# Two graph layers on one core: the first pair of tiles in one written order on four engines, with block-wise products and part of the weight sums on GpSimd

## The chip, the cores and the metric

The kernel runs on one core of a Trainium2 chip. The metric is the time of one execution on the device in microseconds (us), the median of several runs; lower is better. The engines are TensorE (PE), VectorE (DVE), ScalarE (ACT), GpSimd (POOL) and SyncE (SP, which here only issues DMAs). Each engine works through its own list of instructions in order and waits on semaphores for the others.

## The reference

x is 128 graphs of 64 rows with 768 columns, adj is 128 matrices of 64 x 64 zeros and ones. Two layers follow each other; the change touches only the first.

```
h = relu(layernorm(x))
# layer 0, with rels = heads = adj
ctx  = (adj @ (h @ Wadj.T + badj)) / deg + (adj.T @ (h @ Wrev.T + brev)) / rdeg
ctx += h @ Wself.T + bself
agg  = einsum('bij,bijr->bir', adj, E[rels])          # a gather from a table of 80 rows
rel  = agg @ Wr.T + br * deg + (the same with adj.T, E[rr], Wrr, brr)
x = x + ctx + rel
# layer 1
h = relu(layernorm(x))
x = x + gated graph attention of h (six heads of 128) under adj
```

Everything is float32. The gather is computed as a matrix of counts (how often each relation occurs in a row) times a table that already holds E times Wr and Wrr and the bias rows.

## The kernel before

The rows lie in 64 tiles of 128 rows (two graphs each), and two tiles are a pair. Layer 0 runs pair by pair. For each tile the normalised h is multiplied on PE by r, which holds the two scaled adjacencies and an identity: that gives the operands (`operands`, matmuls of line 566, copied out of PSUM by ACT, line 574), 3 blocks of 256 columns for each of the two tiles: a00, a01, a02, a10, a11, a12. They are multiplied by the weights B, a grid of 3 x 3 blocks b00 to b22, each holding its part of Wadj, Wrev and Wself. The result C has 2 x 3 blocks (tile, columns) and is added onto x by DVE (`add`, line 605).

Pair 0 computes C plainly, with 18 products (`PLAIN`); every later pair uses 15 products (`PRODUCTS`) of sums of the operands (f1 to f11, `form`, on DVE) and sums of the blocks of B (g1 to g14, u, v, w, `sum_of_weights`). The sums of B are formed once, while pair 0 runs: 13 operations over 128 x 1536 elements, all on DVE. Some are written over a block of B, and so have to wait until pair 0 is through with it. A product is six matmuls of 128 x 256 (line 613). Four PSUM banks, pwa to pwd, take the products; a bank is free again when DVE has added it onto x.

Around the products there is, for each pair: casting the adjacency (`prep`), degrees through a matmul (`degrees`, line 508) and their reciprocals (`over_degrees`, line 515, line 517 writes r), layer norm (`deviation`: statistics on DVE, the power -1/2 on POOL, line 282; `scaled_mean`, line 286, writes rn; `relu`, line 466, on ACT), the masks for counting (`prep_c`), the counts (`count`, two products over 128 x 1664 and a reduction, `digits`), three copies of them by POOL (line 545), their transposes on PE (`count_t`, line 553, copied out by ACT, line 555), and their product with the table (`counts`, line 597). `build_table` makes the table: `es` is the scaled E, six matmuls (lines 446 and 448) with wrt and the bias rows `bia` and `eb`, a copy by ACT (line 452), a split into three bfloat16 parts on DVE (lines 455 and 457), which DMAs lay into `tab`.

`merged(main, side)` interleaves a pair's list of matmul steps with side work at given step numbers. In layer 0 this gives priorities only: a scheduler in the compiler then orders each engine's instructions, except in a block `tc.manual_schedule(engines=...)`, where the named engines keep the written order. Before the change that holds for DVE alone, in a short stretch at the beginning (the casts and the norms of pair 0). Layer 1 is in a written order for PE, DVE, ACT and POOL (`ORDER`, `END`).

SP issues all loads. Its DMAs and those of ACT's queue share eight semaphores (lanes) in turn, and a DMA is issued only when the previous one of its lane has landed. Before the change the order on SP is: adjacency and x of pair 0, the blocks b00, b10, b20, b01, adjacency and x of pair 1, then b11, b21, b02, b12, b22, then wrt (2 x 384 KB), then the two small rows of `eb`.

Of the kernel before, what the change touches and what calls it, by code (L numbers as in the profile page):

```python
# [71 lines left out]

PLAIN = tuple((f"a{k}{j}", f"b{j}{q}", "abcdab"[2 * q + k], j == 0, f"{k}{q}" if j == 2 else None,
               "+", False) for q in range(3) for j in range(3) for k in range(2))

# [57 lines left out]
def kernel(  # L133
# [85 lines left out]
    def row(v, parts):  # L219

        n = 1
        for s in v.shape:
            n *= s
        return bass.AP(tensor=v.tensor, offset=v.offset, ap=[[0, parts], [1, n]])
# [12 lines left out]


    ident = const.tile([P, P], F32, name="ident")
    make_identity(nc, ident)  # L240
# [61 lines left out]

    def signed(to, s0, x, s1, y):

        if s0 == "-":
            return nc.vector.scalar_tensor_tensor(to, x, -1.0, y, op0=OP.mult,
                                                  op1=OP.add if s1 == "+" else OP.subtract)
        return (nc.vector.tensor_add if s1 == "+" else nc.vector.tensor_sub)(to, x, y)  # L308

# [8 lines left out]

    def sum_of_weights(places, n):
        s0, x, s1, y, at = B_SUMS[n]  # L320
        if at:
            places[n] = places[at]
        return signed(places[n], s0, places[x], s1, places[y])

# [30 lines left out]
    with ExitStack() as px:  # L355
# [5 lines left out]
        X, AI = {}, {}  # L361

        def load(p):
            if p >= NP:
                return
            AI[p] = work.tile([P, 2, 2, N], I32, name="ai")
            for d, src in ((0, adj), (1, adj_t)):
                nc.sync.dma_start(
                    AI[p][:, :, d, :],
                    src[p * 2 * GT : (p + 1) * 2 * GT].rearrange("(t g) i j -> (g i) t j", g=GT))  # L370
            for t in (2 * p, 2 * p + 1):
                X[t] = keep.tile([P, D], F32, name="x", bufs=6)
                nc.sync.dma_start(X[t], xf[t * P : (t + 1) * P, :])

        wrt = [keep.tile([P, D], F32, name="wrt", tag="x", bufs=6) for i in range(2)]
        load(0)
        et = wa.tile([P, NREL], F32, name="et")
        nc.scalar.dma_start(et, e_t)

        bia = keep.tile([5, D], F32, name="bia", tag="hf", bufs=2)  # L380
        for i, v in enumerate((br, brr, badj, brev, bself)):
            nc.scalar.dma_start(bia[i : i + 1, :], row(v, 1))


# [6 lines left out]

        for n in ("b00", "b10", "b20", "b01"):
            load_block(n)
        load(1)
        for n in ("b11", "b21", "b02", "b12", "b22"):
            load_block(n)
        nc.sync.dma_start(wrt[0], wr_t)
        nc.sync.dma_start(wrt[1], wrr_t)
        identb = wa.tile([P, P], BF16, name="identb")
        nc.vector.tensor_copy(identb, ident)  # L400

        blkb = wa.tile([P, P], BF16, name="blkb")
        nc.vector.memset(blkb, 0.0)
        for g in range(GT):
            s = slice(g * N, (g + 1) * N)
            nc.vector.memset(blkb[s, s], 1.0)

        vals = wa.tile([P, NG, N], BF16, name="vals")
        nc.gpsimd.iota(vals, pattern=[[1, NG], [0, N]], base=1, channel_multiplier=0,
                       allow_small_or_imprecise_dtypes=True)  # L410
        rts = []
        for i in range(2):
            r = wa.tile([P, 2, 3, N], F32, name=f"r{i}")
            for k in range(2):
                nc.vector.tensor_copy(r[:, k, 2, :], idc)
            rts.append(r)


        tabs = [wa.tile([3 * (b - a), D], BF16, name=f"tab{a}") for a, b in PARTS]

        def build_table():
            ids = wa.tile([P, NV], F32, name="ids")
            nc.gpsimd.iota(ids, pattern=[[1, NV]], base=1, channel_multiplier=0,
                           allow_small_or_imprecise_dtypes=True)
            es = wa.tile([P, 2, NROW], F32, name="es")
            nc.gpsimd.memset(es, 0.0)
            for d in range(2):
                nc.vector.tensor_mul(es[:, d, d * NV : (d + 1) * NV],
                                     et[:, d * NB + 1 : (d + 1) * NB], ids)


            eb = wa.tile([5, NROW], F32, name="eb")
            nc.gpsimd.memset(eb, 0.0)
            nc.gpsimd.iota(eb[0:1, 0:NV], pattern=[[1, NV]], base=1, channel_multiplier=0,
                           allow_small_or_imprecise_dtypes=True)
            ebr = wa.tile([1, NROW], F32, name="ebr")
            nc.gpsimd.memset(ebr, 0.0)
            nc.gpsimd.iota(ebr[0:1, NV:NCNT], pattern=[[1, NV]], base=1, channel_multiplier=0,
                           allow_small_or_imprecise_dtypes=True)
            nc.sync.dma_start(eb[1:2, :], ebr)  # L440
            nc.sync.dma_start(eb[2:5, NCNT:NROW], ident[0:3, 0:3])
            pt = pss.tile([P, 2, 512], F32, name="pb")
            for hf in range(2):
                s = slice(hf * HALF, (hf + 1) * HALF)
                for d in range(2):
                    nc.tensor.matmul(pt[:NROW, hf, :HALF], es[:, d, :], wrt[d][:, s],
                                     start=(d == 0), stop=False)
                nc.tensor.matmul(pt[:NROW, hf, :HALF], eb, bia[:, s], start=False, stop=True)
            v = keep.tile([P, D], F32, name="tv", tag="hf", bufs=2)
            qs = work.tile([P, 2, D], BF16, name="tq", tag="eq", bufs=1)  # L450
            ql = keep.tile([P, D], BF16, name="tl", tag="hf", bufs=2)
            nc.scalar.copy(v[:NROW].rearrange("p (a b) -> p a b", a=2), pt[:NROW, :, :HALF])
            for i in range(3):
                q = qs[:, i] if i < 2 else ql
                nc.vector.tensor_copy(q[:NROW], v[:NROW])
                if i < 2:
                    nc.vector.tensor_sub(v[:NROW], v[:NROW], q[:NROW])
                for (a, b), tab in zip(PARTS, tabs):
                    nc.sync.dma_start(tab[i : 3 * (b - a) : 3, :], q[a:b, :])
# [58 lines left out]

        def count(p, k):

# [4 lines left out]
            if p < 2 and k == 0:  # L525
                tc.keep_in_program_order(ins)
            nc.vector.tensor_tensor(
                eq, eq, WO[p][:, k, :, None, :].to_broadcast([P, 2, NG, N]), op=OP.mult)
# [55 lines left out]
        def main(p):  # L584
# [43 lines left out]

            rest_of = ["12"] if p else ["12", "01", "11", "10", "00", "02"]
            for i, c in enumerate(rest_of):  # L630
# [56 lines left out]

        with tc.manual_schedule(engines={mybir.EngineType.DVE}):
            prep(0)
            to = [small.tile([P, 2], F32, name="rn") for k in range(2)]  # L690
            mv = [small.tile([P, 2], F32, name="mv") for k in range(2)]
            deviation(X[0], to[0], mv[0])
            rd = degrees(0)
            scaled_mean(to[0], mv[0])
            over_degrees(0, rd)
            deviation(X[1], to[1], mv[1])
            scaled_mean(to[1], mv[1])
        for k in range(2):
            relu(k, to[k])
        operands(0, 0, 0)  # L700
        operands(0, 1, 0)
        prep_c(0)
        late = ([(8 + 6 * i, lambda k=k, q=q: operands(0, k, q)) for i, (k, q) in enumerate(
                    ((0, 1), (1, 1), (0, 2), (1, 2)))]
                + [(20, build_table), (22, lambda: count(0, 0)),
                   (24, lambda: count(0, 1)), (26, lambda: digits(0)),
                   (60, lambda: count_t(0, 0)), (60, lambda: count_t(0, 1))]
                + [(i, lambda n=n: sum_of_weights(bw, n)) for i, n in (
                    (21, "g10"), (38, "u"), (45, "g12"), (50, "g6"), (54, "g14"), (60, "v"), (75, "w"),
                    (85, "g3"), (88, "g9"), (91, "g5"), (94, "g8"), (97, "g1"), (100, "g11"))])  # L710
        for p in range(NP):
            more = [(3, lambda: [f() for k in range(2) for f in finish(p - 1, k)])] if p else late
            if p == 1:
                more.append((10, row_constants))
            if p == NP - 1:
                more += fetch()
            merged(main(p), own(p) + side(p + 1) + more)


    with ExitStack() as px:  # L720
# [366 lines left out]
        def parsed(order):  # L1087
            return [(n, int(k or 0)) for n, _, k in (x.partition("/") for x in order)]

        px.enter_context(tc.manual_schedule(engines={  # L1090
            mybir.EngineType.PE, mybir.EngineType.DVE, mybir.EngineType.Activation,
            mybir.EngineType.Pool}))
        ends = [f for k in range(2) for f in finish(NP - 1, k)]
# [61 lines left out]
```

## Time and profile before

| | |
|---|---|
| median of 5 runs | 2505.07 us (2504.53 to 2505.43) |
| the profiled execution | 2505.43 us |
| its span, first to last instruction | 2503.7 us |
| PE busy | 2465.6 us (98%), 12108 matmul records |
| DVE busy | 1975.4 us (79%) |
| ACT busy | 1073.2 us (43%) |
| POOL busy | 438.2 us (18%) |
| mean granted clock of PE | 0.995 |

A float32 matmul instruction stands as two records. In a timeline row the first number is the start in us from the beginning of the span, the second what the row took, then engine, line, operation, tiles (out <- in), shapes and number of records; in square brackets how long the engine was idle before and what released it. Ends of matmuls are modelled, so starts are the safer numbers there. In rows of windows the columns are: the window, its length, busy time of the engine, its granted clock, the share of the DMA engines' time, GB/s.

### The profile page before, as it was taken

To read this page: it belongs to the slowest core of one execution; us is meant where nothing else is said; L and a number is where in the kernel's file an instruction comes from. 1 tells how busy PE (TensorE), PEld (TensorE's weight loads), DVE (VectorE), ACT (ScalarE), POOL (GpSimd) and SP (SyncE) were. 2 spreads that over 40 slices of the span, in tenths; PEclk is the share of its full clock that TensorE was granted. 3 is DMA by queue.
4 is the path that set the end of the run, shared out by engine and by line. 5 is a ranking of instruction groups with operands and counts; after the bars stand their busy time and mean duration, and the time that the engine had idled before them with its cause. 6 is when DMAs were issued, how large, how long until landed. Compare 5 with 4: busy or idle time off the path is not lost. (4 is left out here: it accounts for less than half of the span.)

```text
span 2503.7 us, 35437 instructions
## 1 busy us (share of the span) xinstructions
PE 2465.6 (98%) x12108; PEld 1731.4 (69%) x12108; DVE 1975.4 (79%) x4112; ACT 1073.2 (43%) x3588; POOL 438.2 (18%) x799
## 2 busy tenths in 40 slices
PE   7999999999999999999999999999999999999997
PEld 5888888888888888888888884444444444444445
DVE  8978677777777776776777655888888888888888
ACT  2222222222222212222222213777777777777777
POOL 0122121121121211211211201111111111111112
PEclk9999999999999999999999999999999999999998
DMA  5122121121121121221211243344444444444434
GB/s 180 55 72 87 53 91 68 53 106 53 53 106 53 67 92 53 88 71 53 103 56 51 102 133 124 96 108 109 113 106 106 108 104 104 108 112 104 104 88 97
DMA packets 116216, 224.58 MB, mean 90 GB/s; under 512 B 36555, under 2 KB 49982, under 8 KB 116035
## 3 DMA queue, kind: packets, MB, share of 16 engines
q1 hardware_dynamic: 106152, 197.48, 24.2%
q0 software_dynamic: 9728, 24.78, 6.2%
q8 instruction: 95, 1.56, 0.3%
q14 instruction: 87, 0.70, 0.1%
q10 hardware_dynamic: 154, 0.06, 0.0%
HBM read 96.07 MB, written 100.66 MB: 79 GB/s over the span
## 5 line engine op out<-in xcount | busy, mean ns | idle before, releaser
L613 PE MATMUL pwa<-weights,op 128*128 128x256 f32 x2304 | 541.7, 382 | 1.1 <-DVE x L605 1.1
L613 PEld LDWEIGHTS pwa<-weights,op 128*128 128x128 f32 x2304 | 423.2, 190 | 69.1 <-DVE x L605 9.0
L574 ACT COPY op<-pb 128x768 f32<-128x768 f32 x160 | 124.2, 797 | 752.7 <-PE pb L566 752.7
L613 PE MATMUL pwb<-weights,op 128*128 128x256 f32 x1536 | 369.5, 381 | 0.0
L308 DVE TENSOR_TENSOR op<-op 128x768 f32<-128x768 f32 x248 | 231.6, 954 | 154.4 <-ACT op L574 154.3
L613 PEld LDWEIGHTS pwb<-weights,op 128*128 128x128 f32 x1536 | 284.5, 190 | 45.6 <-issue 7.0
L806 PE MATMUL pma<-weights,op_f 128*128 128x512 f32 x620 | 308.6, 595 | 1.9 <-DVE weights L833 1.9
L858 ACT ACTIVATE pr<-pr 128x128 f32<-128x128 f32 x768 | 225.3, 296 | 25.3 <-DVE pr L848 25.2
L282 POOL TENSOR_TENSOR rn<-ve,mhalf 128x1 f32<-128x1 f32 x128 | 107.1, 837 | 489.6 <-DVE ve L281 489.6
L806 PE MATMUL pmb<-weights,op_f 128*128 128x512 f32 x372 | 191.7, 597 | 0.0
L806 PEld LDWEIGHTS pma<-weights,op_f 128*128 128x128 f32 x620 | 112.2, 191 | 114.7 <-issue 104.5
L613 PE MATMUL pwc<-weights,op 128*128 128x256 f32 x780 | 187.1, 383 | 0.0
L613 PE MATMUL pwd<-weights,op 128*128 128x256 f32 x768 | 178.4, 381 | 0.0
L566 PE MATMUL pb<-r,h 64*128 64x192 f32 x1536 | 155.4, 341 | 10.2 <-DVE r L517 6.9
L613 PEld LDWEIGHTS pwc<-weights,op 128*128 128x128 f32 x780 | 145.8, 190 | 25.2 <-issue 6.7
L545 POOL COPY c<-cnt 128x243 bf16<-128x243 bf16 x64 | 44.9, 730 | 663.2 <-PE pb L553 598.7
L613 PEld LDWEIGHTS pwd<-weights,op 128*128 128x128 f32 x768 | 146.3, 191 | 20.3 <-issue 0.7
L566 PEld LDWEIGHTS pb<-r,h 64*128 64x128 f32 x1536 | 125.2, 189 | 46.4 <-issue 41.9
L276 DVE BATCH_NORM_STATS2 st<-x 128x6 f32<-128x384 f32 x256 | 134.7, 548 | 28.3 <-DMA x<-in_x_dram 27.1
L643 ACT ACTIVATE hf<-x,rn 128x768 f32<-128x768 f32 x64 | 65.8, 1027 | 192.7 <-issue 128.3
L858 ACT ACTIVATION_READ_ACCUMULATOR pr<-pr 128x1 f32 x768 | 144.2, 188 | 0.0
L645 POOL TENSOR_TENSOR x<-x,hf 128x768 f32<-128x768 f32 x64 | 115.9, 1811 | 92.7 <-ACT hf L643 92.6
(207 smaller groups left out, 4284.5 us busy)
## 6 DMA issues: line engine op xcount, KB each, us to landing
x<-in_x_dram SPq DMA_DIRECT2D x64, 384.0 KB
h<-hf SPq DMA_DIRECT2D x64, 384.0 KB
out_dram<-x SPq DMA_DIRECT2D x64, 384.0 KB
hh<-hh SPq DMA_DIRECT2D x64, 384.0 KB
h<-h SPq DMA_DIRECT2D x64, 384.0 KB
x<-hh SPq DMA_DIRECT2D x64, 384.0 KB
out_dram<-f POOLq DMA_DIRECT2D x62, 384.0 KB, 4.9
hx<-weights SPq DMA_DIRECT2D x88, 192.0 KB
```

Of the source, the lines that this page charges most:

```text
L276: ins = nc.vector.bn_stats(st[:, i, :], src[:, i * HALF : (i + 1) * HALF])
L282: nc.gpsimd.tensor_tensor(to[:, 0:1], ve, mhalf, op=OP.pow)
L308: return (nc.vector.tensor_add if s1 == "+" else nc.vector.tensor_sub)(to, x, y)
L545: nc.gpsimd.tensor_copy(c3, CNT[p][:, k, :, None].to_broadcast([P, NROW, 3]))
L566: nc.tensor.matmul(ps[:, g, i * 3 * N : (i + 1) * 3 * N], H0[t][s, kb * P : (kb + 1) * P], rts[p % 2][s, k].rearrange("p s n -> p (s n)"), ...
L574: nc.scalar.copy(a.rearrange("p h s (g n) -> p g (h s) n", g=GT), ps[:, :, : 6 * N].rearrange("p g (x n) -> p g x n", n=N))
L613: nc.tensor.matmul(bank[b][:, :CQ], OPS[p, an][:, q, s, :], bw[bn][:, (s * KQ + q) * CQ : (s * KQ + q + 1) * CQ], start=(first and q == s ...
L643: nc.scalar.activation(h, X[t], AF.Relu, scale=to[:, 0:1], bias=to[:, 1:2])
L645: nc.gpsimd.tensor_add(X[t], X[t], h)
L806: nc.tensor.matmul(bank[p, b], OPS[p, an][:, q, :], bw2[bn][:, 2 * q * CQ : 2 * (q + 1) * CQ], start=(first and q == 0), stop=(q == KQ - 1 ...
L858: nc.scalar.activation(PR[t][:, j, h, :], PR[t][:, j, h, :], AF.Copy, accum_out=to)
```

## The change

It concerns the time until pair 0 of layer 0 is done.

- PE, DVE, ACT and POOL keep the written order from the kernel's first instruction until pair 0's list is through (`written`), in place of the scheduler's.
- `PLAIN` goes block of C by block of C (00, 10, 02, 12, 01, 11); four blocks get their counts with the products and two, 00 and 10, at the end.
- SP's order of loads is new: x of tile 0, wrt, three of the bias rows, wrt, b00, x of tile 1, b10, b20, b02, b12, pair 1's adjacency and x, b22, b01, b11, b21. The adjacency of pair 0, E and two bias rows go through ACT's queue, and there the two small DMAs for `eb` as well, ahead of ACT's table load.
- The table's six matmuls stand before the first product, in three steps between the first two sets of operands; the copy by ACT follows; the split on DVE stands at step 20.
- Six of the 13 sums of B (g10, w, g6, g14, v, g11) are formed by POOL, seven stay on DVE.
- Pair 1's preparation stands at written steps of pair 0's list (`first`) instead of `side(1)`.

From the 249th instruction of PE on (in pair 1's sixth and seventh product) both kernels have the same list of PE instructions.

```diff
-PLAIN = tuple((f"a{k}{j}", f"b{j}{q}", "abcdab"[2 * q + k], j == 0, f"{k}{q}" if j == 2 else None,
-               "+", False) for q in range(3) for j in range(3) for k in range(2))
+PLAIN = tuple((f"a{k}{j}", f"b{j}{q}", "abcdab"[2 * i + k], j == 0, f"{k}{q}" if j == 2 else None,
+               "+", i > 0) for i, q in enumerate((0, 2, 1)) for k in range(2) for j in range(3))
...
+    in_order = {mybir.EngineType.PE, mybir.EngineType.DVE, mybir.EngineType.Activation,
+                mybir.EngineType.Pool}
+    written = ctx.enter_context(ExitStack())
+    written.enter_context(tc.manual_schedule(engines=in_order))
...
-    def sum_of_weights(places, n):
+    def sum_of_weights(places, n, eng=None):
...
+        load_x(0)
+        load_adj(0, nc.scalar)
+        nc.scalar.dma_start(et, e_t)
+        nc.sync.dma_start(wrt[0], wr_t)
+        for i in range(3):
+            load_bias(i, nc.sync)
+        for i in range(3, 5):
+            load_bias(i, nc.scalar)
+        nc.sync.dma_start(wrt[1], wrr_t)
+        load_block("b00")
+        load_x(1)
+        for n in ("b10", "b20", "b02", "b12"):
             load_block(n)
         load(1)
-        for n in ("b11", "b21", "b02", "b12", "b22"):
+        for n in ("b22", "b01", "b11", "b21"):
             load_block(n)
...
+        nc.scalar.dma_start(eb[2:5, NCNT:NROW], ident[0:3, 0:3])
+        nc.scalar.dma_start(eb[1:2, :], ebr)
...
-            rest_of = ["12"] if p else ["12", "01", "11", "10", "00", "02"]
+            rest_of = ["12"] if p else ["00", "10"]
...
+        prep(0)
+        to, mv = deviations((0,))
+        rd = degrees(0)
+        scaled_rows()
+        mean_and_relu(0, to[0], mv[0])
+        over_degrees(0, rd)
+        table_product(0)
         operands(0, 0, 0)
-        operands(0, 1, 0)
+        table_product(1)
+        table_product(2)
+        table_copy()
+        operands(0, 0, 1)
         prep_c(0)
...
+        first = [
+            (0, lambda: count(0, 0, lambda: mean_and_relu(1, to[0], mv[0]))),
+            (4, lambda: operands(0, 0, 2)),
+            (6, lambda: weights_by(nc.gpsimd, "g10")),
+            (12, lambda: operands(0, 1, 0)),
+            (12, lambda: operands(0, 1, 1)),
+            (14, lambda: count(0, 1)),
+            (20, table_split),
+            (22, lambda: operands(0, 1, 2)),
+            (24, lambda: digits(0)),
+            (27, lambda: prep(1)),
+            (28, norms_1),
+            (29, lambda: DEG.update({1: degrees(1)})),
+            (30, lambda: [mean_and_relu(2 + k, dev["to"][k], dev["mv"][k]) for k in range(2)]),
+            (31, lambda: over_degrees(1, DEG[1])),
+            (32, lambda: weights_by(nc.gpsimd, "w")),
+            (40, lambda: weights_by(nc.vector, "u")),
+            (41, lambda: [count_t(0, k) for k in range(2)]),
+            (42, lambda: weights_by(nc.gpsimd, "g6", "g14", "v")),
+            (42, lambda: prep_c(1)),
+            (44, lambda: weights_by(nc.vector, "g12")),
+            (48, lambda: count(1, 0)),
+            (54, lambda: operands(1, 1, 2)),
+            (54, lambda: operands(1, 1, 1)),
+            (58, lambda: count(1, 1)),
+            (66, lambda: weights_by(nc.vector, "g5", "g3")),
+            (68, lambda: weights_by(nc.gpsimd, "g11")),
+            (70, lambda: operands(1, 0, 0)),
+            (70, lambda: digits(1)),
+            (70, lambda: operands(1, 0, 2)),
+            (74, lambda: weights_by(nc.vector, "g8")),
+            (80, lambda: form(1, "f1", "f7", "f4")),
+            (86, lambda: operands(1, 1, 0)),
+            (86, lambda: operands(1, 0, 1)),
+            (94, lambda: form(1, "f8", "f9", "f2")),
+            (98, lambda: [count_t(1, k) for k in range(2)]),
+            (60, lambda: load(2)),
+            (109, lambda: weights_by(nc.vector, "g9", "g1"))]
...
         for p in range(NP):
-            more = [(3, lambda: [f() for k in range(2) for f in finish(p - 1, k)])] if p else late
+            more = [(3, lambda: [f() for k in range(2) for f in finish(p - 1, k)])] if p else first
...
-            merged(main(p), own(p) + side(p + 1) + more)
+            merged(main(p), own(p) + (side(p + 1) if p else []) + more)
+            written.close()
```

`count(p, k, between)` calls `between` after its first DVE operation, so that the scale and the relu of tile 1 stand there. `signed` and `sum_of_weights` take the engine as an argument.

## The prediction

> **What bounds the kernel now.** I read the page's slices first, then TensorE's (PE's) waits, then its order of time.
>
> ```profile
> PE   7999999999999999999999999999999999999997
> ...
> DVE  8978677777777776776777655888888888888888
> ```
>
> PE is full from the second slice on (a slice is 62.6 us), so a gain must come from what PE loses in the first. These are its waits in the first 120 us, the longest first (waiter, releaser, total us):
>
> ```profile
> PE pb L566 <- DVE r L517: 6.9, 1, 6.9
> PE pb L508 <- DVE ab L480: 4.1, 1, 4.1
> PE pb L553 <- POOL c L545: 3.3, 1, 3.3
> PE pb L566 <- ACT h L466: 3.2, 1, 3.2
> ```
>
> From 120 to 1300 us there is one more, of 1.1 us. In order of time (start, us):
>
> ```profile
> 11.40 1.65 PE L566 MATMUL pb<-r,h 64*128 64x192 f32 x8 [6.95 <-DVE r L517]
> 16.26 1.65 PE L566 MATMUL pb<-r,h 64*128 64x192 f32 x8 [3.21 <-ACT h L466]
> 17.85 3.77 PE L613 MATMUL pwa<-weights,op 128*128 128x256 f32 x12
> ...
> 59.38 1.03 PE L613 MATMUL pwd<-weights,op 128*128 128x256 f32 x4
> 63.67 0.27 PE L553 MATMUL pb<-identb,c 128*126 128x128 bf16 x1 [3.26 <-POOL c L545]
> ...
> 71.31 2.75 PE L613 MATMUL pwa<-weights,op 128*128 128x256 f32 x12
> ...
> 104.73 2.75 PE L613 MATMUL pwa<-weights,op 128*128 128x256 f32 x12
> ```
>
> A product is 6 instructions (12 records) and takes 2.59 us from start to start (71.31 to 73.90), 0.432 each. At 17.85 it took 3.60, and after the gap at 60 the rows run at half speed until 71: the granted clock there is 0.50.
>
> ```profile
> 66.00:67.00 1.00, 1.00 (x5) 0.50 0.00 0
> ```
>
> **The yardstick.** In the built lists of PE both kernels hold the same work up to their 249th instruction, and from there the same order to the end. That place is the row at 104.73. So the change is worth 104.73 minus the time at which the changed kernel gets there, as long as nothing later than PE ends last.
>
> **Opening.** x of tile 0 is now issued first on SP (0.74, was 1.75); statistics started 3.6 us after the issue (1.75 to 5.34), so about 4.4. The adjacency goes to ScalarE's queue at the same 0.73 and shares the engines with x; it was cast 2.7 after its issue, I take 3.9. From statistics to the normalisation's scale took 2.3 us (5.34 to 7.65): 6.7. Reciprocal 1.75 and two products 0.49 give r at 9.0. ScalarE must first issue two tiny DMAs that wait for wrt's landing (issued 1.25; the second x landed 4.3 after its issue behind the first, which is 5.5) at 0.75 and 0.94 (their rows on SP), then load its table 1.28 and do the relu 1.03: 9.5. PE meanwhile does two table products at half speed, 2 x 1.3 (0.65 at full, rows at 32.47 and 33.12), from 7.0 to 9.6. Operands 1.65 to 11.3; four more table matmuls of 0.65 to 0.8, the clock rising at 12.3: 14.6; the copy of the table (0.8) frees the bank: 15.5; operands 0.75: first product at 16.3, against 17.85. The clock needed 3.5 us of work at 16.26 and 6.8 at 64.1 (to 70.9); from 7.0 that is 10.5 to 13.8, so the first product lies between 15.4 and 17.1.
>
> The Trainium skill ("TensorE: Matmul & The Clock Gate", Part 1) has a free-running window of about 3.4 us that must be busy before the clock doubles. By its shortest case the sum falls 0.8 us.
>
> **Three blocks.** P0 to P2 (3 x 2.59) and three sets of operands (2.25) put the end of block 00 at 26.3. In the written order VectorE's (DVE's) add of this block stands ahead of all that follows on DVE: by 23.7 DVE has done both counts of pair 0 (from 12.3; g10 holds it from 13.8 to 17.2, as shown below; then 0.9, 1.8, 0.9, 0.9, 1.8), stands idle 2.8 us, and adds at 26.5.
>
> **DVE and POOL from there.** Six sums leave DVE, 6 x 1.67 = 10.0 us by this group's spacing:
>
> ```profile
> L308 DVE TENSOR_TENSOR weights<-weights 128x1536 f32<-128x1536 f32 x11 | 19.2, 1747 | 0.1
> ```
>
> The trace has no sum of 1536 on POOL. Its add of 128x768 takes 1.81 and its subtraction of 128x18 (L871) 0.24: 0.24 + 1518 x 2.09 ns = 3.42; twice the 1.81 is 3.62. I take 3.42. What it does to DVE is in two rows:
>
> ```profile
> 97.21 1.82 POOL L645 TENSOR_TENSOR x<-x,hf 128x768 f32<-128x768 f32 x1
> 97.26 1.78 DVE L286 SCALAR_TENSOR_TENSOR rn<-mv,rn 128x1 f32<-128x1 f32 x1 [0.40 <-POOL rn L282]
> ```
>
> The scale takes 0.16 elsewhere; here it ends with POOL's add. POOL went from its power to the add before DVE had seen the power done. Line 517 says the same (min/median/max ns):
>
> ```profile
> L517 DVE TENSOR_TENSOR r<-af,rd x64: 271/282/1739, 10.8 to 1429.4; 128x128 f32<-128x128 f32 x64
> ```
>
> Statistics, reductions, reciprocals and adds out of PSUM keep their times beside the same add. So a DVE operation with two SBUF inputs waits out a POOL sum. With that, DVE from 26.5, by rows:
> - add 0.3, table split 3.6, digits 0.7, casts 0.5, two normalisations 2.7, degrees and the wait for the power 0.8: 35.1.
> - w starts as the power ends, as above, and holds the scale of tile 3; g6 follows and holds r; the reciprocal hides beside it: 6.9, to 42.0.
> - r, an add, u (g14 waits for it): 2.5, to 44.5.
> - g14 and v back to back, only short masks between: 7.2, to 51.7.
> - rest of the masks 0.8, g12 1.67, two counts and an add 7.7, g5 and g3 3.3: 65.2.
> - g11 was waiting: 3.4, to 68.7, digits beside it.
> - g8 1.7, two copies by POOL 0.7, f1, f7, f4 2.6, add of block 01 0.5: 74.1.
>
> DVE is held 13.9 us here for the 10.0 it gave away. The add of 01 frees the bank for pair 1's first product, and PE, which stands there from 70.9 by its own list, starts it at 74.1. PE's stop at the transposes (37.1 to 39.9, behind the relu of tile 3 on ScalarE) lies inside that slack. After it 46 product instructions (19.9), eight count matmuls, three transposes and a degree (1.3) and one wait of 1.7 for the add of block 11, queued behind pair 2's masks: 97.0.
>
> **The sum.** 104.73 - 97.0 = 7.7; off the profiled time of 2505.43 (span 2503.7, 1.7 around it) that is 2497.7; the median shown is 0.36 lower: 2497.4. What is moved on SP costs nothing: wrt goes ahead of the weights (2 x 1.1 us at 350 GB/s), but b21, the last, then lands near 31.6 and is first read at 38.6; b00, due at 16.3, lands near 10 (x, adjacency, both wrt and b00 are 2.1 MB from 2.0 on, with some 2 us of the queue waiting for its lanes). These 6 us are the cover; without it PE would wait from there. Of the six blocks counted after the last product, four are now counted with their products: the same work, no saving.
>
> The Trainium skill ("SBUF — State Buffer", Who interferes with whom) counts copies, casts and scalar operations in fast modes among those that block; no row here has one beside a POOL add. With them the sum gets 0.7 us worse.
>
> **Rivals.**
> B. DVE is held less than the rows say, because its queue has unblocked work to do or POOL's reads leave room. Without any hold the same list ends at 89.6, PE alone deciding: 15.1 less, 2490. For it: some of line 517's 64 stand at 282 ns. Against: every late one ends with POOL's add.
> C. The gain is handed back in line: POOL goes from w to g6 without letting the scale of tile 3 in. The relu is then 3.4 late, PE's stop at the transposes becomes 6.2, and the clock halves for up to 6.8 us as after the gap at 60 (3.4 lost). The slack of 3.3 before pair 1 covers half: 3.5 to 5 worse, about 2502.5, not to be told from before. For it: POOL's step from power to add with no gap. Against: DVE, asking first, should come between.
> D. Slower: the POOL sum itself. Every further microsecond of one sum moves the end by five (w, g6, g14, v, g11 in the list above). At 4.9 us the gain is gone, at 5.9 the time is 2510. For it: no row has this shape, and POOL's copy of counts grows from 0.39 to 1.15 when it meets DVE. Against: all 64 adds took 1.80 to 1.83.
>
> **How the numbers follow.** 0.2%, about what a measurement can tell from no change, is 5.0 us: 2500.1. Forecast 0.47, at 2497.4, own range 2494 to 2501 (clock 0.9 each way, POOL sum 3.62: 1.0, blocked casts 0.7, landings 0.6). B 0.18, C 0.22, D 0.13. Faster: 0.42 of the forecast, B, 0.03 of C: 0.63. Same: 0.05, 0.19 of C: 0.24. Slower: D. The range reaches to B and C, with little left out: 2489 to 2507.
>
> **What would show it.** First product near 16.3; DVE idle before the add of block 00; six POOL sums of 3.4 with a DVE two-input operation stretched beside each; PE waiting at the transposes for some 3 us near 37, and for a DVE add near 71; the row of 104.73 at 97. It is wrong if DVE's rows keep their lengths beside POOL's sums, if these take 5 us, or if PE is late at that row although DVE was in time.

## The result: no faster, some 3 us slower

| | before | after |
|---|---|---|
| median | 2506.74 us (49 runs) | 2509.68 us (29 runs, 2505.48 to 2512.83) |
| ratio to before, 95% interval | | 1.0013 (1.0008 to 1.0018) |
| the profiled execution, its span | 2505.43, 2503.7 us | 2512.83, 2511.0 us |

The forecast was 2497.4 us, 5 us or more faster than before with a chance of 0.63. The time is 2.7 us above the upper end of its range, and within the 0.2% that were called "about no change", on the slow side. The profiled execution is the longest of the 29, so its 7.3 us over the span of before are more than the 2.9 us between the medians. Numbers of lines have moved by 6 to 32: 566 is 598 now, 574 606, 605 637, 607 639, 613 645, 553 585, 555 587, 286 292, 517 547; 308 is 315, 534 566, 645 677.

The page's slices of the changed kernel, of which only the first can have changed much:

```profile
PE   8899999999999999999999999999999999999997
...
DVE  8977677677777776776777655888888888888888
```

PE's waits of the changed kernel in the first 120 us (waiter, releaser, total, times, longest):

```profile
PE pb L538 <- DVE ab L510: 6.2, 1, 6.2
PE pwa L645 <- DVE x L637: 3.1, 1, 3.1
PE pb L585 <- ACT cntT L587: 2.9, 2, 2.5
PE pwa L645 <- DVE x L639: 2.1, 1, 2.1
PE pwb L645 <- DVE x L637: 1.9, 1, 1.9
PE pwb L645 <- DVE x L639: 1.8, 1, 1.8
PE pb L471 <- DVE es L462: 1.4, 1, 1.4
```

The waits for r, h and c are gone. Behind those of the opening (ab and es) stand five others, four of which are for additions and subtractions (637, 639) by which DVE empties a bank of PSUM. In order of time, PE of the changed kernel (start, us, in brackets the wait):

```profile
16.89 1.99 PE L645 MATMUL pwa<-weights,op 128*128 128x256 f32 x8
...
77.16 0.70 PE L645 MATMUL pwa<-weights,op 128*128 128x256 f32 x2 [3.10 <-DVE x L637]
...
87.15 1.56 PE L645 MATMUL pwb<-weights,op 128*128 128x256 f32 x6 [1.86 <-DVE x L637]
...
99.05 2.86 PE L645 MATMUL pwb<-weights,op 128*128 128x256 f32 x12 [1.80 <-DVE x L639]
...
104.84 4.25 PE L645 MATMUL pwa<-weights,op 128*128 128x256 f32 x12 [2.08 <-DVE x L639]
...
139.81 4.54 PE L645 MATMUL pwa<-weights,op 128*128 128x256 f32 x12 [1.68 <-DVE x L637]
```

The first product is 1 us earlier than before, pair 1's first product stands at 77.16, and the yardstick place (104.73 before) is reached at 104.84: the whole gain is gone there. The last two rows took 4.25 and 4.54 us in place of 2.75: after both stops PE ran at half clock for 3.4 us. What comes of it by the end of pair 2 is read from the row with which ScalarE copies the first operands of pair 3 ("pair 3's row" from here on; before, then changed):

```profile
157.28 0.80 ACT L574 COPY op<-pb 128x768 f32<-128x768 f32 x1 [13.94 <-PE pb L566]
```

```profile
162.42 0.80 ACT L606 COPY op<-pb 128x768 f32<-128x768 f32 x1 [15.61 <-PE pb L598]
```

So 0.1 us is lost up to the yardstick and 5.0 more by the end of pair 2, 1.4 at the border of the layers (PE at half clock for 6.8 us there, 3.4 before) and the rest at the end. Of the 5.0, 3.5 are the two stretches at half clock (the rows from 104.84 to 111.04 took 1.8 us more than the same rows before, those from 139.81 to 144.19 took 1.7 more), and the rest is longer waits. Of the other 28 executions only the mean clock is on record, so it isn't shown how much of the 2.9 us between the medians lies there.

What DVE did beside five of POOL's sums in the changed kernel (the sixth, g10, had held the scale of tile 1 before that, 3.38 us from 15.61):

```profile
36.61 3.38 DVE L292 SCALAR_TENSOR_TENSOR rn<-mv,rn 128x1 f32<-128x1 f32 x1 [0.27 <-POOL rn L288]
...
42.00 1.71 DVE L547 TENSOR_TENSOR r<-af,rd 128x128 f32<-128x128 f32 x2
...
45.96 3.34 DVE L272 TENSOR_SCALAR bb<-bb 128x128 f32<-128x128 f32 x1
49.22 3.42 DVE L519 TENSOR_SCALAR cnt<-dg 128x4 bf16<-128x4 f32 x1
...
67.51 3.42 DVE L566 CAST si<-sum 128x52 int32<-128x52 f32 x1
```

Of the five long ones only the first two have two operands in SBUF. The sums themselves took what was forecast, except one that met a DVE sum (min/median/max ns, x6):

```profile
L315 POOL TENSOR_TENSOR weights<-weights x6: 3425/3430/4822, 15.5 to 66.1; 128x1536 f32<-128x1536 f32 x6
```

### The profile page after: what moved, and what is told of

Same layout as the page of the kernel before. It is cut to its first block, busy times and chain, and to the rows that moved or that the text cites. A ratio compares the mean times of both kernels' runs of the same rounds, so it can differ in the third digit from the quotient of the medians.

```text
span 2511.0 us, 35432 instructions
## 1 busy us (share of the span) xinstructions
PE 2469.9 (98%) x12108; PEld 1732.4 (69%) x12108; DVE 1983.8 (79%) x4102; ACT 1073.4 (43%) x3588; POOL 461.7 (18%) x805
```

## The experiments

Theories when they began: H, POOL's sums hold DVE longer than DVE would need for them, and the late DVE is why PE waits for banks in pair 1. W, the waits in pair 1 come from the order of DVE's list there, whoever forms the sums.

### 1. All sums on DVE

```diff
-            (6, lambda: weights_by(nc.gpsimd, "g10")),
+            (6, lambda: weights_by(nc.vector, "g10")),
...
```

The lines of w, g6, g14, v and g11 are changed in the same way.

> The changed kernel with its six POOL sums formed by DVE at the same places of the written list; all else as changed. Theory H (POOL's sums hold DVE longer than DVE would need for them, and the late DVE makes PE wait in pair 1): between 27.8 and 76.7 us of the changed kernel DVE was held by 3.2 (scale of tile 3), 2.9 (r), 3.2 (bb), 3.3 (cnt) and 3.2 us (si), 15.9 in all; five sums on DVE are 5 x 1.74 = 8.7. So the add of block 01 comes 7 us earlier (69 to 71 in place of 76.7), PE's stop of 2.9 us at the transposes is gone, the waits of 1.8 and 2.1 us for banks b and a in pair 1 are gone or below 0.5 each, and the row that stood at 104.8 stands at 96 to 99. Time 2499, 2496 to 2502; ratio to before 0.996 to 0.998. Rival W (the written order itself makes DVE late, by pair 2's norms falling beside pair 1's adds, whoever forms the sums): both bank waits stay at 1.5 us or more, the row stands at 103 or later, ratio 1.000 or above.

The time is 2503.36 us, ratio to before 0.9991 (0.9983 to 1.0000): 6.3 us faster than the changed kernel, but above the 2496 to 2502 of H. PE's waits in order of time:

```profile
71.78 0.70 PE L645 MATMUL pwa<-weights,op 128*128 128x256 f32 x2 [1.72 <-DVE x L637]
...
81.77 1.56 PE L645 MATMUL pwb<-weights,op 128*128 128x256 f32 x6 [1.86 <-DVE x L637]
...
93.67 2.86 PE L645 MATMUL pwb<-weights,op 128*128 128x256 f32 x12 [1.80 <-DVE x L639]
...
99.46 2.86 PE L645 MATMUL pwa<-weights,op 128*128 128x256 f32 x12 [2.07 <-DVE x L639]
...
128.54 4.54 PE L645 MATMUL pwa<-weights,op 128*128 128x256 f32 x12 [1.91 <-DVE x L639]
```

Each theory has one half. The yardstick row moved from 104.84 to 99.46, nearly as H had it (96 to 99). But the waits of 1.80 and 2.07 us are the same to 0.01 us, though DVE came 5.4 us earlier, as W had it. And of the 5.3 us gained at the yardstick against before, only 2.0 are left at the row of pair 3 (155.24).

The account of DVE between its add of block 00 and its add of block 01 closes: 27.78 to 76.69 in the changed kernel (48.9 us), 27.23 to 71.31 here (44.1). In the changed kernel the scale of tile 3, r, bb, cnt and si (DVE's five rows in the section on the result) took 3.22, 1.23, 3.13, 3.25 and 3.24 us more than here: 14.1. Here five sums took 5 x 1.67 = 8.4, and DVE waited 0.8 for a load. 14.1 - 8.4 - 0.8 = 4.9, of 4.8 measured.

### 2. The hold by itself

The kernel does nothing but this: for each of 18 forms two operations alone, then a small memset that lets one POOL sum of 128x1536 start, and the form again 3 to 8 times, on tiles that the sum doesn't touch:

```
    for n, f in forms:
        f()
        f()
        v.memset(pa[:, 0:1], 1.0)
        for i in range(n):
            f()
        nc.gpsimd.tensor_add(pc, pa, pb)
        v.tensor_copy(s26[:, 0:1], pc[:, 0:1])
```

The last copy lets DVE wait for the sum before the next form.

> Not the computation of the reference (x is copied to the output): 18 forms of DVE operations of this kernel, each run twice alone and then 3 to 8 times beside one POOL sum of 128x1536, and ScalarE's relu beside another. Theory H (every DVE operation that reads and writes SBUF through its fast copy, cast and scalar forms waits as the two-input ones do): besides the two-input products and scalar_tensor_tensor also tensor_scalar f32 128x128, tensor_scalar 128x4, the casts and tensor_scalar bf16 show one instance of 2.5 to 3.4 us. Reduce, bn_stats, bn_aggr, reciprocal and the forms with a PSUM operand keep their time within 0.1 us. Rival N (the rule of the prediction): only forms with two SBUF operands show such an instance, and the 3.3 us of bb, cnt and si in the changed kernel were waits for something else. ScalarE's relu keeps 1.03 under both. The POOL sum takes 3.4 where it holds DVE, more where DVE holds it.

Some of DVE's groups beside a POOL sum:

```profile
13.45 4.16 DVE L93 TENSOR_SCALAR f<-f 128x128 f32<-128x128 f32 x4
...
23.19 4.49 DVE L95 CAST i<-f 128x52 int32<-128x52 f32 x6
...
38.23 4.68 DVE L98 TENSOR_SCALAR h<-h 128x256 bf16<-128x256 bf16 x6
...
57.98 2.71 DVE L101 TENSOR_TENSOR f<-ps,f 128x256 f32<-128x256 f32 x6
...
67.12 2.69 DVE L103 TENSOR_REDUCE d<-f 128x4 f32<-128x256 f32 x6
...
84.21 5.33 DVE L105 RECIPROCAL f<-f 128x256 f32<-128x256 f32 x3
...
103.26 4.34 DVE L109 SCALAR_TENSOR_TENSOR rn<-d,rn 128x1 f32<-128x1 f32 x6
```

Alone, two of them took 0.48, 0.40, 0.49, 0.87, 0.86, 3.53 and 0.34 us. So the group of line 93 is 4 x 0.24 = 0.96 plus 3.2, that of line 95 6 x 0.20 plus 3.3, that of line 98 plus 3.2, that of line 109 plus 3.3: one operation of each, 3.37 us long, waited for about the whole sum (3.42). Casts between float32, bfloat16 and int32, tensor_scalar on 128x4 and the two-input forms in bfloat16 lost 3.1 to 3.4 as well. Additions and maxima with an operand in PSUM, reductions, reciprocal, bn_stats and bn_aggr lost 0.1 or less, a group of eight memsets 0.4 (none of them longer than 0.27), ScalarE's relu nothing (0.86 alone and beside). In the kernel before, a tensor_scalar on 128x1 (line 281) runs 30 times beside one of POOL's adds, and none takes more than 0.16 us; on 128x4 one waited for the sum here. The first form, the product of two float32 operands, shows nothing here: POOL's sum began only behind its last operation. H holds, N falls. The Trainium skill ("SBUF — State Buffer", Who interferes with whom) lists copies, casts and tensor_scalar in their two-port modes, and two SBUF inputs; these runs agree with it, and the forecast should have gone by it.

### 3. The six sums left out

```diff
             for n in names:
-                sum_of_weights(bw, n, eng)
+                if eng is nc.vector:
+                    sum_of_weights(bw, n, eng)
+                elif B_SUMS[n][4]:
+                    bw[n] = bw[B_SUMS[n][4]]
...
+        for n, m in (("g10", "b10"), ("g6", "b10"), ("w", "b01"), ("g14", "b21"), ("v", "b11")):
+            load_block(m, n)
```

Pair 1 and all later pairs then multiply by other weights.

> The changed kernel without the six sums that POOL formed: their places are filled by plain loads of blocks of the weights, so pair 1 and later use other weights; the other seven sums stay on DVE. It shows what is left of the first 110 us when these sums cost no engine anything. Theory H: another 8.7 to 10.4 us of DVE less than with all sums on DVE, but PE's own list then decides: add of 01 before PE has got there, the row of 104.8 at 90 to 93, time 2493, 2490 to 2497. Rival W: bank waits of 1.5 us or more stay in pair 1, row at 98 or later, time above 2499.

The time is 2504.05 us (ratio 0.9991, 0.9981 to 1.0000), not the 2493 of H, and the yardstick row stands at 99.12, as W had it (98 or later). But the loads that fill the places of the sums (0.8 MB each, issued behind all the others) had pushed back the table's DMAs, so PE stood 1.90 us at 47.68 and ran at half clock for 3.4 us after it. The next kernel is the same with four of the five loads issued at step 36 of pair 0's list, in place of the end of the first loads:

> e2_no_six_sums with the loads that fill the places of the missing sums issued later, behind the table's DMAs, so that PE doesn't wait for the table at 47.7. DVE has 10.4 us less to do than in e1, all of it before pair 1's products; pair 1 and later use other weights. Theory D: DVE stands idle for PE before pair 1, PE reaches pair 1's first product at 68 to 70 with no wait, and from there DVE's list takes as long as in e1: the row that stood at 99.5 at 95 to 97, that of 155.2 at 151 to 153.5, time 2500, 2498 to 2502.5. If only the six sums' DVE time counted, all rows would stand 10 us earlier than in e1; if they did not count at all, as in e1.

The time is 2501.44 us (0.9977, 0.9968 to 0.9986), and the rows are within 0.1 us of where theory D (of the next section) put them: yardstick 94.94, pair 3's row 151.11. So 10.4 us less work for DVE than in experiment 1 moved the yardstick by 4.5. Before pair 1 DVE stands idle for PE (first row; the second is read below):

```profile
66.78 0.42 DVE L638 TENSOR_TENSOR x<-pwa,x 128x256 f32<-128x256 f32 x1 [4.42 <-PE pwa L630]
...
94.47 0.41 DVE L640 TENSOR_TENSOR x<-x,pwa 128x256 f32<-128x256 f32 x1
```

and PE then waits for banks b and a again:

```profile
89.15 2.86 PE L646 MATMUL pwb<-weights,op 128*128 128x256 f32 x12 [1.12 <-DVE x L640]
...
94.94 4.54 PE L646 MATMUL pwa<-weights,op 128*128 128x256 f32 x12 [2.07 <-DVE x L640]
```

DVE's two rows are the start and the end of its list from the add of block 01 to the subtraction that frees bank a for the yardstick product. It took 94.47 - 66.78 = 27.69 us. In experiment 1 these rows stand at 71.31 and 98.99 (27.68), in the changed kernel at 76.69 and 104.38 (27.69):

```profile
76.69 0.42 DVE L637 TENSOR_TENSOR x<-pwa,x 128x256 f32<-128x256 f32 x1
...
104.38 0.41 DVE L639 TENSOR_TENSOR x<-x,pwa 128x256 f32<-128x256 f32 x1
```

Whenever DVE begins this stretch, it needs 27.7 us for it in this order, and the product starts 0.47 later.

### 4. The order of that stretch

Theories from here on: O, the two waits (1.80 and 2.07 us) come from the place of the subtractions in DVE's list. D (not the prediction's rival of that letter): DVE, without a pause from 28 us on, sets the pace until pair 2 is done, and what PE gains before is waited for there. In `more`, the closing of pair 0 (the norms of its new x, `finish`) is handed over later in pair 1's list:

```diff
-            more = [(3, lambda: [f() for k in range(2) for f in finish(p - 1, k)])] if p else first
+            more = [(30 if p == 1 else 3, lambda: [f() for k in range(2) for f in finish(p - 1, k)])] if p else first
```

This is done on the kernel of experiment 1, on the changed kernel, and on the kernel before.

> All thirteen sums on DVE as in e1_all_on_dve, and in pair 1 the closing of pair 0 (norms of its new x, finish) is handed to the scheduler at step 30 of the pair's list in place of step 3. In DVE's list the subtractions for bank b and bank a of pair 1 then stand ahead of these norms, the first also ahead of the reciprocal. Theory O (the two bank waits come from the place of these subtractions in DVE's list, behind pair 0's closing norms and POOL's additions; not from how much DVE has to do before): the waits of 1.80 and 2.07 us are each below 0.5, the row that stood at 99.5 stands at 95.5 to 96.5, time 2499.5, 2497 to 2502, ratio to before 0.997. Rival D (DVE is the engine that sets the pace through pair 2, and whatever PE gains is waited for there): the row of pair 2 that stood at 155.2 in e1 stands no more than 1 us earlier, its wait of 1.9 at 128.5 grows to 4 or 5, time 2502.5 to 2504. Rival H alone (late DVE): it had fallen for these waits in e1, since they kept their length to 0.01 us though DVE was 5 us earlier.

> The changed kernel, six sums on POOL, with the same late closing of pair 0 in pair 1. Theory O with H for the rest: the waits of 1.8 and 2.1 at 99 and 104.8 are gone, the row of 104.8 stands at 100.5 to 102, some 5 us behind e5; time 2505, 2503 to 2507, ratio 0.999 to 1.000. If POOL's sums were no loss by themselves, it stands level with e5 within 1 us. Rival D: time as the changed kernel, 2508 to 2510.

> The kernel before with the late closing of pair 0 in pair 1 and nothing else changed. Theory O: PE had no bank wait there, so nothing is gained; the row of 104.7 stays within 0.3 us, time the same within 0.1%. If it gains 2 us or more, the late closing helps by itself (in pair 2, where the kernel before waits 1.07), and what e5 gains over e1 can't all be put down to the two waits.

With all sums on DVE both waits are gone, and the yardstick is reached at 96.52, 3 us earlier than in experiment 1. The time is 2505.48 (0.9995, 0.9987 to 1.0004), no better, and above what either theory had. PE's waits behind the yardstick:

```profile
118.77 2.86 PE L645 MATMUL pwa<-weights,op 128*128 128x256 f32 x12 [0.90 <-DVE x L637]
...
124.58 0.22 PE L585 MATMUL pb<-identb,c 128*126 128x128 bf16 x1 [2.04 <-ACT op L606]
...
127.33 0.43 PE L585 MATMUL pb<-identb,c 128*117 128x128 bf16 x2 [2.04 <-ACT cntT L587]
...
136.32 2.86 PE L645 MATMUL pwa<-weights,op 128*128 128x256 f32 x12 [1.20 <-DVE x L637]
```

These are 6.2 us of waits, two of them for ScalarE, whose copies there stand behind the relu of pair 3 (122.82 and 126.10), which waits for DVE's scales; and PE ran 6.8 us at half clock there. Pair 3's row stands at 157.24. O was right about where the two waits come from, and D about what taking them away is worth, though not about where it is lost (one wait of 4 to 5 us). On the changed kernel the time is 2509.27 (1.0009, 1.0000 to 1.0018), again 3.8 us more than with the sums on DVE, and the yardstick is reached at 99.57, 3.1 us behind it, where O with H had some 5. On the kernel before it is 2508.81 (1.0007, 0.9998 to 1.0016): nothing gained, the yardstick 1.0 us later (105.73) and pair 3's row 3.7 us later. That kernel had neither of the two waits, so the late closing costs 2.7 us behind the yardstick by itself, and of the 4.9 us lost there with all sums on DVE not all need be PE's gain waited for.

### 5. Less work for DVE in pairs 1 and 2

On the kernel of experiment 1 the counts of pairs 2 and 3 are left out, and their digits are made of pair 1's sums:

```diff
         def count(p, k, between=None):
+            if p in (2, 3):
+                return
...
-            SUM[p] = work.tile([P, 2, 2, NG], F32, name="sum")
+            SUM[p] = SUM[1] if p in (2, 3) else work.tile([P, 2, 2, NG], F32, name="sum")
```

> All thirteen sums on DVE as in e1_all_on_dve, and the counts of pairs 2 and 3 (two masks' products and a reduction for each of their four tiles) left out; their digits are made of pair 1's sums, so the counts of pairs 2 and 3 are wrong. DVE has 7.8 us less to do in pair 1's and again in pair 2's time; PE's list is that of e1. Theory D (DVE, full from 28 to 135 us, sets the pace until pair 2 is done, so that what PE gains before is waited for there): bank a's wait of 2.07 at 99.5 gone or below 0.8, the wait of 1.91 at 128.5 and the half clock after it gone, the row of pair 3 that stood at 155.2 in e1 (157.3 before) stands at 149 to 151.5, time 2498 to 2501. Rival L (latency: the waits come from chains through POOL's powers, ScalarE and the order of the lists, not from how much DVE does): the waits keep their lengths within 0.5, the row stands at 154 or later, time 2502 or more.

The time is 2499.91 us (0.9967, 0.9955 to 0.9980). The waits of 2.07 and 1.91 are gone, pair 3's row stands at 151.14. PE's waits after 60 us:

```profile
73.93 1.22 PE L647 MATMUL pwa<-weights,op 128*128 128x256 f32 x2 [4.69 <-DVE x L639]
...
96.26 2.86 PE L647 MATMUL pwb<-weights,op 128*128 128x256 f32 x12 [1.76 <-DVE x L641]
```

The first is longer than in experiment 1: the digits of pairs 2 and 3 now stand ahead of that add in DVE's list (1.1 us), and DVE came to pair 1's digits 1.1 us later. PE runs 6.8 us at half clock there; all the same pair 2 ends 4.1 us earlier. D holds, though only 4.1 of the 15.6 us of work left out are seen at pair 3's row: between 28 and 140 us DVE now waits 5.5 us for loads of x, 3.9 for ScalarE and 1.3 for PE. L is right about the wait of 1.8 alone, which has the reciprocal and the norms ahead of it and no counts.

### 6. g10 alone on POOL

This is the kernel of experiment 1 with `(6, lambda: weights_by(nc.gpsimd, "g10"))`.

> The changed kernel with one sum, g10, left on POOL and the five others formed by DVE. In the changed kernel g10 held the scale of tile 1 for 3.2 us, and DVE stood idle for 1.9 us before the add of block 00; on DVE the sum takes 1.74. Theory H: hold and sum both lie beside DVE's idle time before that add, so every row stands within 0.5 us of e1's, time as e1 within 0.1% (2502.5 to 2504.5). If each POOL sum by itself cost what six cost together (6.3 / 6), it would be 1 us slower than e1.

The time is 2505.49 us (0.9994, 0.9985 to 1.0003) against 2503.36. In the trace the yardstick row stands at 99.80 (99.46 with all on DVE), as H had it; behind it PE ran at half clock twice for 3.4 us, where it did so once, and pair 3's row stands at 157.59, 2.4 us later, which H didn't have. The medians differ by 2 us with overlapping intervals: whether g10 costs nothing or 1 us is not settled by the times.

### 7. Copies from DVE to ScalarE

If DVE sets the pace, work taken off it without holding it is worth its own time. On the kernel of experiment 1 (the mark that kept pair 2's cast in its place of the list falls away with it):

```diff
-            ins = nc.vector.tensor_copy(af, AI[p])
+            early = 1 <= p <= 3
+            ins = (nc.scalar.copy if early else nc.vector.tensor_copy)(af, AI[p])
...
-            nc.vector.tensor_copy(ab, af)
+            (nc.scalar.copy if early else nc.vector.tensor_copy)(ab, af)
...
-                nc.vector.tensor_copy(q[:NROW], v[:NROW])
+                (nc.vector.tensor_copy if i < 2 else nc.scalar.copy)(q[:NROW], v[:NROW])
...
-            nc.vector.tensor_copy(
+            (nc.scalar.copy if p < 3 else nc.vector.tensor_copy)(
                 CNT[p][:, :, :NCNT].rearrange("p k (d v) -> p k d v", d=2),
```

The second kernel has this edit as well; the third doesn't have it, but has the six sums on `nc.gpsimd` again:

```diff
-            more = [(3, lambda: [f() for k in range(2) for f in finish(p - 1, k)])] if p else first
+            more = [(12 if p == 1 else 3, lambda: [f() for k in range(2) for f in finish(p - 1, k)])] if p else first
```

> All thirteen sums on DVE as in e1_all_on_dve, and for the first pairs some copies moved from DVE to ScalarE: the casts of the adjacency of pairs 1 to 3 (0.29 + 0.29 each), the cast of the counts of pairs 0 to 2 (0.24 each) and the third cast of the table (0.56); 3.0 us in all before pair 2 is done. The scheduler then also puts the subtraction for bank b of pair 1 ahead of the reciprocal and that for bank a ahead of the counts. Theory D (DVE sets the pace until pair 2 is done): the row of pair 3 that stood at 155.2 in e1 stands 3 to 5 us earlier, at 150 to 152.5, the time is 2500.5, 2498 to 2502.5. Rival A (ScalarE is the next that is late: its copies of operands and of the transposed counts come behind the casts): waits of PE for ScalarE of 1 us or more between 60 and 130, row at 154 or later, time as e1 or worse.

> As e15_casts_on_act, and the closing of pair 0 handed over at step 12 of pair 1's list in place of step 3. Theory D: what is gained in pair 1 by order alone is given back in pair 2, so the row of pair 3 stands within 1 us of e15's, time within 0.1% of it. If it stands 2 us or more earlier, the order of the lists has a share of its own.

> The kernel of e15_casts_on_act with the six sums back on POOL, as in the changed kernel. Theory H with D (a POOL sum holds DVE for about 3.3 us where DVE would need 1.74 for it, and DVE sets the pace): DVE is held by some 12 us between 28 and 77 us (the scale of tile 3, r, two small operations of pair 1's masks, the casts of the counts) for 8.7 us of sums, PE waits 4 us or more for the add of block 01, the row of pair 3 that stood at 149.6 in e15 stands at 153 to 156, time 2504 to 2507, ratio to before 0.999 to 1.000. Rival (the loss of the changed kernel against e1 came from its bad place in the lists, which the scheduler has now mended): row within 1 us of e15's, time 2500 to 2502.

The first takes 2500.94 us (0.9978, 0.9969 to 0.9987), with pair 3's row at 149.59, and of PE's waits after 70 us these are left:

```profile
82.51 2.05 PE L646 MATMUL pwb<-weights,op 128*128 128x256 f32 x6 [3.08 <-DVE x L638]
...
128.66 2.86 PE L646 MATMUL pwa<-weights,op 128*128 128x256 f32 x12 [0.53 <-DVE x L638]
```

Rival A's wait for ScalarE is there once, 1.14 us at 64.91, but the row and the time are D's. Pair 3's row is 5.7 us earlier than in experiment 1 for 3.0 us of copies: the scheduler's new order, without the waits of 1.80 and 2.07 us at banks b and a, must have a share, and the two weren't tried apart.

The second, with the closing of pair 0 at step 12, takes 2498.48 us (0.9974, 0.9963 to 0.9985), with pair 3's row at 149.88, within 0.3 of the first. The intervals overlap. Both beat both kernels: they are 5 to 8 us below the kernel before and 9 to 11 below the changed one.

The third, with POOL's six sums back, takes 2510.59 us (1.0013, 1.0004 to 1.0022), with pair 3's row at 161.00. The rival (the new order mends the loss) falls. H and D had 2504 to 2507 and 153 to 156, so the direction is theirs and the size is not. PE's waits show how it grew:

```profile
44.79 0.26 PE L586 MATMUL pb<-identb,c 128*117 128x128 bf16 x1 [5.38 <-ACT cntT L588]
...
85.60 1.22 PE L646 MATMUL pwa<-weights,op 128*128 128x256 f32 x2 [7.35 <-DVE x L638]
```

ScalarE's list has the cast of pair 2's adjacency ahead of a copy of the transposed counts. Here the cast ran at 44.00, when DVE's reduction dg (43.52 to 43.93) had read the tile it writes; and dg stood in DVE's list behind the products for r, which took 1.96 us under POOL's sum, an add and u. So a hold of DVE passed through ScalarE to PE. And the scheduler has put pair 2's masks and counts ahead of the add of block 01, which came at 85.12, 13.8 us later than in experiment 1. How the excess divides between the two wasn't tried.

## Why the prediction was wrong, step by step

**Opening.** This part was right. The adjacency landed later than taken (cast 5.53, not 3.9), r was done at 10.5 in place of 9.0, and the first product started at 16.89 (16.3 forecast, 15.4 to 17.1 as its range). The add of block 00 came at 27.78 (26.5), so 1.3 us of lateness start here.

**POOL's sums.** Their length was right (3.43, forecast 3.42), and with it rival D's mechanism falls: the longest, 4.82, had met a DVE sum, the others took 3.43. That the time lies next to the 2510 of rival D is chance. Rival B falls too, since every sum held DVE, and rival C: the scale of tile 3 ended with w, at 39.99, without waiting for g6 too, and PE stood 2.48 and 0.41 us at the transposes (2.8 forecast).

**What they hold.** The rule (two SBUF inputs) was too narrow, but it cost little in the sum: the stretch of g14 and v was already written as lost, and the digits of pair 1, thought to run beside g11, were held for 3.4 us and followed it. The hold as a whole was sized well (13.9 us forecast, 14.1 measured), but the 10.0 us that DVE "gave away" for it count six sums, where five stand in that stretch, 8.4 us. With short masks of 1.8 us in place of 0.8, the add of block 01 was 1.8 us later than the late start explains: PE began pair 1 at 77.16, not 74.1.

**From there to the yardstick: the step that failed.** The prediction said that after that add there come 46 product instructions, eight count matmuls, three transposes, a degree and one wait of 1.7, "97.0": PE's list, 22.9 us. DVE's own list over the same stretch was not summed. It is 27.7 us long in three kernels whatever came before (experiments 1 and 3): eight forms, two sums, pair 2's masks, four norms with 2.5 us of waits for POOL's powers, the reciprocal and most of a count, with the subtractions that free banks b and a behind most of it. 77.16 + 27.7 is the yardstick row, 104.84, and that alone is 4.8 of the 7.8 us by which the prediction missed it; the late start of pair 1 is the other 3.1. The one wait that was forecast, 1.7 us for the add of block 11, was there with 1.86; the waits for banks b and a, 1.80 and 2.08 us, were put at nothing, and they are 3.9 of the 4.8. PE's own list was sized well: with the closing norms moved out of DVE's way (experiment 4) PE took 23.6 us for it, 72.94 to 96.52.

**The yardstick itself.** From the 249th instruction on both kernels have PE's list in common, but not DVE's state. The prediction let a gain there count in full, "as long as nothing later than PE ends last". Something later did: from 28 to 140 us DVE in the changed kernel waited for neither PE nor ScalarE, only for POOL's powers (3.8 us), and PE's gain of 5.3 us in experiment 1 was 2.0 at pair 3's row. The changed kernel, with no gain to hand back, lost 5.0 more there in its profile, 3.5 of them at half clock. So the sum was built on the wrong engine: from 28 us until pair 2 is done DVE sets the pace, five of the sums moved to POOL gave it 8.4 us before pair 1 and took 14.1, and the rest of the change could only bring what it took off DVE.

**Written order, block by block, table ahead.** They were no loss, and hardly a gain: experiment 1 is the change without POOL's sums, and it is 0.9991 (0.9983 to 1.0000) of before.

## What to carry to other kernels

Sum the list of every engine, not only that of the busiest, over the stretch that a change is to shorten: the slice table shows PE at 90% and more and DVE at 80%, and yet it was DVE's list that PE waited for in pairs 1 and 2. A sum of 128x1536 on POOL is no gift to DVE where DVE works from SBUF beside it: the hold (3.1 to 3.4 us for the operation that met a whole sum) is longer than DVE's own 1.67. And when PE arrives earlier at one place, look for the same wait at the next place where that engine must answer; what moved the end was work taken off the late engine (the counts of two pairs, or 3 us of copies to ScalarE with the new order that came with them), and with POOL's sums beside them the copies moved nothing (2510.59).

## What the runs showed of the hardware

Stretches at half clock were 3.4, 6.8 or 10.2 us long in every trace but where the span's end cuts one, and a stop of the same length was followed by one or not: behind the waits of 1.80 and 2.07 us PE ran 3.4 us at half clock in the changed kernel, and not in experiment 1 (window, length, busy time, granted clock, DMA share, GB/s; the changed kernel, then experiment 1):

```profile
100.00:112.00 12.00, 9.93 (x45) 0.86 0.61 231
```

```profile
90.00:104.00 14.00, 10.13 (x47) 1.00 0.59 225
```

The Trainium skill ("TensorE: Matmul & The Clock Gate", Part 1) has a window of 3.4 us that runs on its own; the lengths agree. If a stop is followed by such a stretch in some executions only, the times of one kernel should come in steps, and 28 of the 29 times of the changed kernel lie in groups near 2507.7, 2510.2 and 2512.4 (the other is 2505.48). That these groups are numbers of such stretches was not shown, and it can hardly be all of it: the mean clocks of the executions, kept to three digits, average 0.9943 in the first group and 0.9936 in the last, which over 2510 us is an estimated 1.6 of the 4.8 us between them.
